# The neighbours' running count by TensorE (row blocks transposed, then multiplied by a constant staircase) in place of a VectorE scan

## The chip, the cores and the metric

The kernel runs on one core of one Trainium2 chip. The metric is the device time of one execution in microseconds (us). TensorE is called PE below, its weight loads PEld, VectorE DVE, ScalarE ACT, GpSimdE POOL; SP and ACT also issue DMAs. Every engine works off its own list of instructions in the order in which the program was built; it never overtakes an instruction that waits.

## The reference, cut to what matters

Sixteen graphs (batch 16) of 1024 nodes with 64 channels go through four graph layers with residuals. `adj` is a float 0/1 matrix per graph. Only layer 0 matters here: it drops some neighbours of a node by their rank, then takes quantiles over the remaining ones.

```python
neigh = (adj_ > 0) & ~eye
ni = neigh.astype(jnp.int32)
rank = jnp.cumsum(ni, axis=-1) - ni            # the running count along a row
nb = ni.sum(-1)
skip = jnp.where(nb > T, (nb + K - 1) // K, 1) # T, K = 10, 2
rem = neigh & (sk > 1) & (rank % sk == sk - 1) & mask[:, :, None]
rem = rem | jnp.swapaxes(rem, 1, 2)
adj_d = jnp.where(rem, 0.0, adj_)              # the neighbours that stay
s = jnp.sort(jnp.where((adj_d > 0)[..., None], x[:, None, :, :], jnp.inf), axis=2)
# agg: weighted quantiles 0.25, 0.5, 0.75 of s, then two dense layers; layers 1 to 3 use the full adj
```

## The kernel before, in words

The graphs are worked through in eight pairs. Of each pair there are five kinds of work:

- **Sort** (`sort_pair`, L720 to L803): the nodes' values are sorted on DVE in 55 compare steps (L729, L736, L737, called *forward steps* here), and 55 *back steps* (L753, L754, L756/L757 or L760) carry codes back to the nodes. The masks between go through DRAM (L740, L749).
- **Preparation** (`neighbours`, L806 to L904): for each graph eight row blocks of 128 nodes, in two halves of four. A block is loaded (L819), compared with 0 into `ni` (fp8, L820), its diagonal cleared by POOL (L821), counted along the row by a scan (`cum`, L825), and the raw block is transposed on PE and stored for the later layers (L831 to L834). After four blocks a chain of ten small DVE instructions (`sk`, L840 to L850) gives each row's skip. Then per block three ACT passes over 1024 columns (L854 Square with the bias `sk[:, 2]`, L855 Square, L856 Relu) give `rem`, 0/1; PE adds up `ni`, `-rem` and `-rem` transposed into `ndT` (L875), and ACT evicts (L881). Every PE result of the preparation goes through two PSUM buffers, `pk`. `ni`, `rem` and `wide` have one buffer, so a pair's second graph starts when its first is through. At the end of a graph PE counts the neighbours that stay (L885) and ten small DVE instructions (L892 to L904) make the quantiles' positions.
- **Selection** (`weights`, `select`): PE multiplies `ndT` by tables made from the sort (`wt`, L921; `comb`, L1043), ACT evicts (L1051, L1098), DVE finds maxima (L1109 to L1122), PE and DVE pick the values (L1143, L1151).
- **Extras** (`extras`): nodes with too many neighbours, until L1315.
- **Layers** (`layers`): the rest of layer 0 and layers 1 to 3 of both graphs, until L1528 and L1530 of each graph.

The program order of the loop is: selection of pair p; extras of p; layers of p; preparation of p+1; sort of p+1; load and normalisation for p+2. A scheduler in the language layer decides the order within each engine's list when the program is built; it may move the sort of a later pair ahead, since its buffers are its own. Selection uses all PSUM banks, so it doesn't overlap the preparation, whose `pk` needs two of them. The selection of p+1 needs `ndT` and the positions of p+1, and `wt`, which follows the sort.

So the trace falls into *mixed* stretches M0 to M8 (preparation with extras and layers; M0 is the start, M8 the end) and *selection* stretches S1 to S8 between them. I let S begin at its first L1043 and end at its last L1143.

Of the kernel before, what the change touches and what calls it, by code (L numbers as in the profile page):

```python
# [42 lines left out]
def gnn_stack(ctx, tc, x, adj, nodemask, w, out):  # L43
# [22 lines left out]
    nc.vector.tensor_copy(ident_b, ident)  # L66
    offdiag = const.tile([P, P], BF16, name="offdiag")
    nc.vector.tensor_scalar(offdiag, ident, -1.0, 1.0, op0=ALU.mult, op1=ALU.add)
    ones_b = const.tile([P, N], BF16, name="ones_b")
    nc.vector.memset(ones_b, 1.0)  # L70
    ones_row = const.tile([1, P], F32, name="ones_row")
    nc.vector.memset(ones_row, 1.0)
# [51 lines left out]
    with tc.tile_pool(name="cd", bufs=1, side="right") as cd:  # L124
        code0 = cd.tile([P, N], U16, name="code0")
        rk = cd.tile([P, N], I32, name="rk")
        nc.gpsimd.iota(rk, pattern=[[1, 32], [32, 32]], base=0, channel_multiplier=0)
        rf = cd.tile([P, N], F32, name="rf")
        nc.vector.tensor_copy(rf, rk)
        wf = cd.tile([P, N], F32, name="wf")  # L130
        nc.vector.tensor_scalar(wf, rf, 1.0 / WL, 0.5 / WL - 0.5, op0=ALU.mult, op1=ALU.add)
        wi = cd.tile([P, N], I32, name="wi")
        nc.vector.tensor_copy(wi, wf)
        nc.vector.tensor_copy(wf, wi)
        nc.vector.scalar_tensor_tensor(rf, wf, float(CODE - WL), rf, op0=ALU.mult, op1=ALU.add)
        nc.vector.tensor_copy(code0, rf)
        nc.sync.dma_start(c0_d, code0)
    halfdown = const.tile([P, 1], F32, name="halfdown")
    nc.vector.memset(halfdown, -1023.5 / 2048.0)

# [308 lines left out]
    def general(gw):  # L449
# [47 lines left out]
        with tc.For_i(0, B, 1) as b:  # L497
            with ExitStack() as per_batch:
# [13 lines left out]
                with (  # L512
                    tc.tile_pool(name="nb1", bufs=1) as nb1,
                    tc.tile_pool(name="nb2", bufs=2) as nb2,
                    tc.tile_pool(name="nbp", bufs=2, space=PSUM) as nbp,
                ):
                    kept = nb1.tile([P, NT, N], BF16, name="kept")
                    notrem = nb1.tile([P, NT, N], BF16, name="notrem")
                    for t in range(NT):
                        a = nb2.tile([P, N], F32, name="a", bufs=3)  # L520
                        nc.sync.dma_start(a, adj[ds(b, 1), t * P : (t + 1) * P, :].rearrange("o p j -> (o p) j"))
                        for q in range(0, NT, 4):
                            pt = nbp.tile([P, 4, P], F32, name="pt")
                            for k in range(4):
                                nc.tensor.transpose(pt[:, k, :], a[:, (q + k) * P : (q + k + 1) * P], ident)
                            nc.scalar.copy(adjT[:, q : q + 4, t * P : (t + 1) * P], pt)
                        ni = nb2.tile([P, N], BF16, name="ni")
                        nc.vector.tensor_single_scalar(ni, a, 0.0, op=ALU.is_gt)
                        nc.vector.tensor_mul(ni[:, t * P : (t + 1) * P], ni[:, t * P : (t + 1) * P], offdiag)
                        cum = nb2.tile([P, N], F32, name="cum")  # L530
                        nc.vector.tensor_tensor_scan(cum, ones_b, ni, 0.0, op0=ALU.mult, op1=ALU.add)

                        nbi = nb2.tile([P, 1], I32, name="nbi")
                        nc.vector.tensor_scalar_add(nbi, cum[:, N - 1 : N], 1.0)
                        nc.vector.tensor_single_scalar(nbi, nbi, 1, op=ALU.logical_shift_right)
                        act = nb2.tile([P, 1], F32, name="act")
                        nc.vector.tensor_scalar(
                            act, cum[:, N - 1 : N], MAX_DEGREE, mask[:, t : t + 1], op0=ALU.is_gt, op1=ALU.mult
                        )
                        sk = nb2.tile([P, 2], F32, name="sk")  # L540
                        nc.vector.tensor_copy(sk[:, 1:2], nbi)
                        nc.vector.scalar_tensor_tensor(sk[:, 0:1], sk[:, 1:2], 1.0, act, op0=ALU.add, op1=ALU.mult)
                        nc.vector.tensor_scalar_add(sk[:, 0:1], sk[:, 0:1], -1.0)
                        nc.vector.tensor_scalar_mul(sk[:, 1:2], sk[:, 0:1], 2.0)
                        r1 = nb2.tile([P, N], BF16, name="r1")
                        nc.vector.tensor_scalar(r1, cum, sk[:, 0:1], None, op0=ALU.is_equal)
                        rem = nb2.tile([P, N], BF16, name="rem")
                        nc.vector.scalar_tensor_tensor(rem, cum, sk[:, 1:2], r1, op0=ALU.is_equal, op1=ALU.add)
                        nc.vector.tensor_mul(rem, rem, ni)
                        nc.vector.tensor_sub(kept[:, t, :], ni, rem)  # L550
                        nc.vector.tensor_scalar(notrem[:, t, :], rem, -1.0, 1.0, op0=ALU.mult, op1=ALU.add)
                    for t in range(NT):
                        at = slice(t * P, (t + 1) * P)
                        pk = nbp.tile([P, NT, P], BF16, name="pk")
                        for j in range(NT):
                            nc.tensor.transpose(pk[:, j, :], kept[:, t, j * P : (j + 1) * P], ident_b)
                        nc.vector.tensor_mul(ndT[:, :, at], pk, notrem[:, :, at])
                        nc.vector.tensor_add(ndT[:, t, at], ndT[:, t, at], ident_b)
                    pn = nbp.tile([P, NT], F32, name="pn", bufs=1)
                    for t in range(NT):  # L560
                        for j in range(NT):
                            nc.tensor.matmul(
                                pn[:, t : t + 1], ndT[:, j, t * P : (t + 1) * P], ones_b[:, 0:1],
                                start=(j == 0), stop=(j == NT - 1),
                            )
                    for k, tau in enumerate(TAUS):
                        nc.vector.tensor_scalar(pos1[:, :, k], pn, tau, 1.0 - tau, op0=ALU.mult, op1=ALU.add)
# [237 lines left out]
    def neighbours(b, ndT, row10, qb, qz, nb, nbp):  # L805
# [7 lines left out]
        ni = wide[:, :, pad:]  # L813
        rem = nb.tile([P, NT, N], F8, name="rem")
        for t0 in range(0, NT, HT):
            cum = nb.tile([P, HT, N], F16, name="cum")
            for t in range(t0, t0 + HT):
                a = nb.tile([P, N], F32, name="a", bufs=2)
                nc.sync.dma_start(a, adj[b, t * P : (t + 1) * P, :])  # L819
                nc.vector.tensor_single_scalar(ni[:, t, :], a, 0.0, op=ALU.is_gt, saturate=False)  # L820
                nc.gpsimd.tensor_mul(  # L821
                    ni[:, t, t * P : (t + 1) * P], ni[:, t, t * P : (t + 1) * P], offdiag, saturate=False
                )

                nc.vector.tensor_tensor_scan(  # L825
                    cum[:, t - t0, :], ni[:, t, :], wide[:, t, pad - 1 : pad - 1 + N], 0.0, op0=ALU.add, op1=ALU.add
                )
                for q in range(0, NT, 4):
                    pt = nbp.tile([P, 4, P], F32, name="pk")
                    for k in range(4):  # L830
                        nc.tensor.transpose(pt[:, k, :], a[:, (q + k) * P : (q + k + 1) * P], ident)  # L831
                    at = nb.tile([P, 4, P], F32, name="at", bufs=3)
                    nc.scalar.copy(at, pt)  # L833
                    nc.scalar.dma_start(  # L834
                        a_d[b % 4, q : q + 4, :, t * P : (t + 1) * P].rearrange("j p n -> p j n"), at
                    )


            sk = nb.tile([P, 4, HT], F32, name="sk")
            nc.vector.tensor_tensor(sk[:, 2, :], cum[:, :, N - 1], ni[:, t0 : t0 + HT, N - 1], op=ALU.add)  # L840
            nbi = nb.tile([P, HT], I32, name="nbi")
            nc.vector.tensor_scalar_add(nbi, sk[:, 2, :], 2.0)
            nc.vector.tensor_single_scalar(nbi, nbi, 2, op=ALU.logical_shift_right)
# [2 lines left out]
            nc.vector.tensor_copy(sk[:, 1, :], nbi)  # L846
            nc.vector.scalar_tensor_tensor(sk[:, 1, :], sk[:, 1, :], 1.0, sk[:, 0, :], op0=ALU.add, op1=ALU.mult)
            nc.vector.tensor_scalar(sk[:, 2, :], sk[:, 1, :], -3.0, 4.0, op0=ALU.mult, op1=ALU.add)
            nc.vector.tensor_scalar_add(sk[:, 1, :], sk[:, 1, :], -1.0)
            nc.vector.scalar_tensor_tensor(sk[:, 3, :], sk[:, 1, :], -1.0, sk[:, 1, :], op0=ALU.mult, op1=ALU.mult)  # L850
            for t in range(t0, t0 + HT):
                k = t - t0
                sq = nb.tile([P, N], F32, name="sq")
                nc.scalar.activation(sq, cum[:, k, :], AF.Square, bias=sk[:, 2, k : k + 1], scale=1.0)  # L854
                nc.scalar.activation(sq, sq, AF.Square, bias=sk[:, 3, k : k + 1], scale=1.0)  # L855
                nc.scalar.activation(rem[:, t, :], sq, AF.Relu, bias=one, scale=-1.0, saturate=False)  # L856

# [791 lines left out]
```

## Time and profile before

| | us |
|---|---|
| median of 3 runs | 5952.29 (5937.49 to 5957.01) |
| the profiled execution, its own time | 5945.84 |
| span of the profiled execution | 5944.1 |
| M0 and S1 | 291.4 and 398.4 |
| M1 to M6, mean | 288.1 |
| S2 to S7, mean | 430.5 |
| M7 and S8 | 273.5 and 399.2 |
| M8 | 270.3 |

How to read it: the span runs from the first to the last instruction of one profiled execution. The stretches add up to the span. S2 to S7 are longer than S1 and S8. M7 is the last stretch that prepares a pair, M8 has extras and layers alone, and S8 has no sort beside it. Over the span DVE is busy 5122.3 us, PE 4397.4, ACT 3817.2 and POOL 181.7.

### The profile page before, as it was taken

To read this page: it belongs to the slowest core of one execution; us is meant where nothing else is said; L and a number is where in the kernel's file an instruction comes from. 1 tells how busy PE (TensorE), PEld (TensorE's weight loads), DVE (VectorE), ACT (ScalarE), POOL (GpSimd) and SP (SyncE) were. 2 spreads that over 40 slices of the span, in tenths; PEclk is the share of its full clock that TensorE was granted. 3 is DMA by queue.
4 is the path that set the end of the run, shared out by engine and by line. 5 is a ranking of instruction groups with operands and counts; after the bars stand their busy time and mean duration, and the time that the engine had idled before them with its cause. 6 is when DMAs were issued, how large, how long until landed. Compare 5 with 4: busy or idle time off the path is not lost. (4 is left out here: it accounts for less than half of the span.)

```text
span 5944.1 us, 114264 instructions
## 1 busy us (share of the span) xinstructions
PE 4397.4 (74%) x45010; PEld 2736.4 (46%) x45010; DVE 5122.3 (86%) x13031; ACT 3817.2 (64%) x5701; POOL 181.7 (3%) x283
## 2 busy tenths in 40 slices
PE   1488677895768858788577885788767886779856
PEld 1355443554435544355434554345443554436542
DVE  9999888998789987999879997798879999567744
ACT  2587647775576855668567665676566776577824
POOL 2000000000000000000000000000000000000000
PEclk5699778997889978899688996899868998789967
DMA  3401364014631146211561115611345013520024
GB/s 126 123 26 37 97 200 127 30 48 120 194 94 34 38 127 212 77 36 44 152 204 55 50 51 150 190 39 48 90 141 172 34 48 97 183 87 19 10 75 139
DMA packets 524419, 568.22 MB, mean 96 GB/s; under 512 B 263808, under 2 KB 413568, under 8 KB 523872
## 3 DMA queue, kind: packets, MB, share of 16 engines
q1 hardware_dynamic: 381472, 476.43, 26.3%
q10 hardware_dynamic: 140064, 81.84, 4.5%
q8 instruction: 355, 5.82, 0.4%
q0 software_dynamic: 2336, 2.57, 0.2%
q14 instruction: 192, 1.57, 0.1%
HBM read 376.95 MB, written 183.76 MB: 94 GB/s over the span
## 5 line engine op out<-in xcount | busy, mean ns | idle before, releaser
L1043 PE MATMUL comb<-wt,ndT 128*128 128x512 fp8e5 x6144 | 1442.3, 387 | 146.7 <-ACT sign L1098 121.7
L1051 ACT ACTIVATE y<-comb,qb 128x512 int16<-128x512 f32 x1152 | 744.1, 718 | 512.4 <-PE comb L1043 510.7
L1043 PEld LDWEIGHTS <-ndT 128*128 128x128 fp8e5 x6144 | 592.5, 99 | 876.8 <-issue 246.3
L1143 PE MATMUL cand<-vtab,sign 128*128 128x48 f16 (+1 forms) x18432 | 669.3, 191 | 54.0 <-DVE agg L1018 36.1
L1143 PEld LDWEIGHTS <-sign 128*128 128x128 fp8e5 x18432 | 645.2, 96 | 111.9 <-issue 51.8
L1098 ACT ACTIVATE sign<-comb,lower 128x1024 fp8e5<-128x1024 int16 (+1 forms) x640 | 696.5, 1088 | 0.0
L1098 ACT ACTIVATE sign<-comb,half 128x1024 fp8e5<-128x1024 int16 (+1 forms) x640 | 691.3, 1080 | 0.0
L1114 DVE TENSOR_TENSOR y<-y 128x512 uint16<-128x512 uint16 (+5 forms) x896 | 672.1, 792 | 8.4 <-PE comb L1096 7.2
L1151 DVE COPY_PREDICATED cand<-w_f,cand 128x256 f32<-128x256 uint16 (+1 forms) x1536 | 535.8, 383 | 75.0 <-PE cand L1143 72.8
L1096 PE MATMUL comb<-ident_b,y 128*128 128x128 bf16 x4608 | 316.9, 222 | 117.2 <-ACT sign L1098 76.8
L833 ACT COPY at<-pk 128x512 f32<-128x512 f32 x256 | 147.5, 586 | 384.5 <-PE pk L831 197.1
L1406 PE MATMUL bank<-adjT,nd 128*64 128x512 f32 x1024 | 307.4, 668 | 90.4 <-DMA adjT<-a_d 88.9
L1096 PEld LDWEIGHTS <-y 128*128 128x128 bf16 x4608 | 292.7, 99 | 145.5 <-issue 144.4
L875 PE MATMUL pk<-minus_b,rem 128*128 128x128 bf16 x1024 | 225.5, 247 | 175.2 <-ACT rem L856 175.1
L1406 PE MATMUL bank<-att,hs 128*64 128x512 f32 x512 | 211.0, 941 | 185.0 <-ACT hs L1522 185.0
L825 DVE TENSOR_TENSOR_SCAN cum<-ni 128x1024 f16<-128x1024 fp8e5 x128 | 295.0, 2306 | 32.6 <-POOL ni L821 23.2
L875 PE MATMUL pk<-ident_b,ni 128*128 128x128 bf16 x1024 | 223.3, 244 | 125.1 <-ACT ndT L881 62.7
L729 DVE TENSOR_TENSOR swapped<-s 128x512 uint16<-128x512 f32 x440 | 302.5, 687 | 5.8 <-ACT s L717 1.6
L737 DVE TENSOR_TENSOR s<-s 128x512 f32<-128x512 f32 (+2 forms) x440 | 289.8, 659 | 0.0
L736 DVE TENSOR_TENSOR s<-s 128x512 f32<-128x512 f32 (+2 forms) x440 | 289.6, 658 | 0.0
L921 DVE TENSOR_SCALAR wt<-node 128x2048 uint8<-128x2048 f16 x224 | 268.0, 1221 | 13.1 <-PE comb L1234 13.0
L831 PE MATMUL pk<-ident,a 128*128 128x128 f32 x1024 | 193.5, 339 | 112.9 <-DMA a<-in_adj_dram 79.8
(323 smaller groups left out, 8258.8 us busy)
## 6 DMA issues: line engine op xcount, KB each, us to landing
adjT<-a_d SPq DMA_DIRECT2D x384, 512.0 KB
a<-in_adj_dram SPq DMA_DIRECT2D x128, 512.0 KB
a_d<-at ACTq DMA_DIRECT2D x256, 256.0 KB
m_d<-swapped SPq DMA_DIRECT2D x104, 512.0 KB
swapped<-m_d SPq DMA_DIRECT2D x104, 512.0 KB
n_d<-nat SPq DMA_DIRECT2D x128, 128.0 KB
x_d<-xr SPq DMA_DIRECT2D x48, 256.0 KB
comb_x<-x_d ACTq DMA_DIRECT2D x24, 512.0 KB
```

The lines of the kernel that those rows point to most:

```text
L729: nc.vector.tensor_tensor(side(swapped[:, k, :], j), hi, lo, op=ALU.is_gt)
L737: nc.vector.tensor_tensor(to_hi, lo, hi, op=ALU.min)
L825: nc.vector.tensor_tensor_scan(cum[:, t - t0, :], ni[:, t, :], wide[:, t, pad - 1 : pad - 1 + N], 0.0, op0=ALU.add, op1=ALU.add)
L875: nc.tensor.matmul(pk[:, n % 4, :], lhs, rhs, start=(n % 4 == 0 and m == 0), stop=(m == len(terms) - 1 and last),)
L1043: nc.tensor.matmul(pw, ndT[:, j, t * P : (t + 1) * P], wt[1 + g8][:, j].rearrange("p w c -> p (w c)"), start=(j == 0), stop=(j == NT - 1),)
L1051: nc.scalar.activation(y[:, 0, chunks, at : at + 8 * d_].rearrange("p q (w d) -> p q w d", d=d_), pw.rearrange("p (w q d) -> p q w d", w=8 ...
L1096: nc.tensor.transpose(pt[:, q - q0, :], y[:, 0, q, :].bitcast(BF16), ident_b)
L1098: nc.scalar.activation(signs[tl][s][:, q0:q1, :], pt.bitcast(I16), AF.Sign, bias=before[s], scale=-1.0, saturate=False,)
L1114: nc.vector.tensor_tensor(v[:, :, :, :n], v[:, :, :, :n], v[:, :, :, n : 2 * n], op=ALU.max)
L1143: nc.tensor.matmul(cand[:, e, at : at + 12 * d_].rearrange("p (d l) -> p d l", l=12), signs[tl][sec][:, chunk, :], tab[:, q, :, half_ * 12 ...
L1151: nc.vector.copy_predicated(v[:, :, :, dst : dst + k], mk.to_broadcast([P, 2, C // 2, k]), v[:, :, :, frm : frm + k])
L1406: nc.tensor.matmul(po[to : to + C, :], lhs, rhs[:, f * HALF : (f + 1) * HALF], start=(j == 0), stop=(j == NT - 1))
```

## The change

The scan goes. The count of a row's neighbours comes from the comparison itself: it is done in two halves of 512 columns, each with an accumulated sum, and the diagonal's own entry is subtracted (a product with the identity, also with an accumulated sum). The running count comes from PE: each 128x128 block of `ni` is transposed by a product with the identity, evicted by ACT to fp8 (`turned`), and multiplied by a constant staircase of 0, 1 and 2, four blocks of a half row accumulating in one PSUM bank. The first Square reads that bank, once for each half row of 512 columns; the second half row's bias also holds the first half's count. `ones_w` and the smaller `ones_b` concern a fallback path (`general`), of which the trace shows nothing running. Two setup instructions and `stairs` are new.

```diff
-            cum = nb.tile([P, HT, N], F16, name="cum")
+            sk = nb.tile([P, 6, HT], F32, name="sk")
             for t in range(t0, t0 + HT):
                 a = nb.tile([P, N], F32, name="a", bufs=2)
                 nc.sync.dma_start(a, adj[b, t * P : (t + 1) * P, :])
-                nc.vector.tensor_single_scalar(ni[:, t, :], a, 0.0, op=ALU.is_gt, saturate=False)
-                nc.gpsimd.tensor_mul(
-                    ni[:, t, t * P : (t + 1) * P], ni[:, t, t * P : (t + 1) * P], offdiag, saturate=False
+                own = ni[:, t, t * P : (t + 1) * P]
+                for h in range(2):
+                    nc.vector.tensor_scalar(
+                        ni[:, t, h * (N // 2) : (h + 1) * (N // 2)], a[:, h * (N // 2) : (h + 1) * (N // 2)], 0.0, 0.0,
+                        op0=ALU.is_gt, op1=ALU.add, accum_out=sk[:, 4 + h, t - t0 : t - t0 + 1], saturate=False,
+                    )
+                eye = nb.tile([P, P], F32, name="eye")
+                nc.vector.scalar_tensor_tensor(
+                    eye, own, 1.0, ident, op0=ALU.mult, op1=ALU.mult, accum_out=sk[:, 3, t - t0 : t - t0 + 1]
                 )
-
-                nc.vector.tensor_tensor_scan(
-                    cum[:, t - t0, :], ni[:, t, :], wide[:, t, pad - 1 : pad - 1 + N], 0.0, op0=ALU.add, op1=ALU.add
-                )
+                nc.gpsimd.tensor_mul(own, own, offdiag, saturate=False)
...
-            sk = nb.tile([P, 4, HT], F32, name="sk")
-            nc.vector.tensor_tensor(sk[:, 2, :], cum[:, :, N - 1], ni[:, t0 : t0 + HT, N - 1], op=ALU.add)
+            own = 4 if t0 == 0 else 5
+            nc.vector.tensor_sub(sk[:, own, :], sk[:, own, :], sk[:, 3, :])
+            nc.vector.tensor_scalar_mul(sk[:, 4:, :], sk[:, 4:, :], 2.0)
+            nc.vector.tensor_add(sk[:, 2, :], sk[:, 4, :], sk[:, 5, :])
...
+            nc.vector.tensor_add(sk[:, 4, :], sk[:, 4, :], sk[:, 2, :])
...
                 sq = nb.tile([P, N], F32, name="sq")
-                nc.scalar.activation(sq, cum[:, k, :], AF.Square, bias=sk[:, 2, k : k + 1], scale=1.0)
+                turned = nb.tile([P, NT, P], F8, name="turned", bufs=2)
+                for q in range(0, NT, 4):
+                    pt = nbp.tile([P, 4, P], F32, name="pk")
+                    for i in range(4):
+                        nc.tensor.matmul(
+                            pt[:, i, :], ni[:, t, (q + i) * P : (q + i + 1) * P], ident_b, start=(i == 0), stop=(i == 3)
+                        )
+                    nc.scalar.activation(turned[:, q : q + 4, :], pt, AF.Copy, saturate=False)
+                for q in range(0, NT, 4):
+                    cum = nbp.tile([P, 4, P], F32, name="pk").rearrange("p k n -> p (k n)")
+                    for j in range(4):
+                        nc.tensor.matmul(
+                            cum[:, j * P :], turned[:, q + j, :], stairs[:, 3 * P : (7 - j) * P],
+                            start=(j == 0), stop=(j == 3),
+                        )
+                    nc.scalar.activation(
+                        sq[:, q * P : (q + 4) * P], cum, AF.Square, bias=sk[:, 2 + q // 2, k : k + 1], scale=1.0
+                    )
                 nc.scalar.activation(sq, sq, AF.Square, bias=sk[:, 3, k : k + 1], scale=1.0)
                 nc.scalar.activation(rem[:, t, :], sq, AF.Relu, bias=one, scale=-1.0, saturate=False)
```

More of the change, by code (lines that the diff above doesn't have):

```diff
@@ L68, in gnn_stack @@
     nc.vector.tensor_scalar(offdiag, ident, -1.0, 1.0, op0=ALU.mult, op1=ALU.add)
-    ones_b = const.tile([P, N], BF16, name="ones_b")
+    ones_b = const.tile([P, P], BF16, name="ones_b")
     nc.vector.memset(ones_b, 1.0)
@@ L137, in gnn_stack @@
         nc.sync.dma_start(c0_d, code0)
+        past_ = cd.tile([P, N], I32, name="past_")
+        nc.gpsimd.iota(past_, pattern=[[1, N]], base=1 - 3 * P, channel_multiplier=-1)
+        stairs = const.tile([P, N], F8, name="stairs")
+        nc.vector.tensor_copy(wf, past_)
+        nc.vector.tensor_scalar(wf, wf, 0.0, 2.0, op0=ALU.max, op1=ALU.min)
+        nc.vector.tensor_copy(stairs, wf, saturate=False)
     halfdown = const.tile([P, 1], F32, name="halfdown")
@@ L518, in general @@
                     notrem = nb1.tile([P, NT, N], BF16, name="notrem")
+                    ones_w = nb1.tile([P, N], BF16, name="ones_w")
+                    nc.vector.memset(ones_w, 1.0)
                     for t in range(NT):
@@ L530, in general @@
                         cum = nb2.tile([P, N], F32, name="cum")
-                        nc.vector.tensor_tensor_scan(cum, ones_b, ni, 0.0, op0=ALU.mult, op1=ALU.add)
+                        nc.vector.tensor_tensor_scan(cum, ones_w, ni, 0.0, op0=ALU.mult, op1=ALU.add)
                         nbi = nb2.tile([P, 1], I32, name="nbi")
```

## The prediction

> **What bounds the kernel now.** I read the page's busy times first, then the same by stretch.
>
> ```profile
> PE 4397.4 (74%) x45010; PEld 2736.4 (46%) x45010; DVE 5122.3 (86%) x13031; ACT 3817.2 (64%) x5701; POOL 181.7 (3%) x283
> ```
>
> DVE leads, but only as an average. The windows view, cut at S1, M4, S5, M7, S8 and M8 (columns: stretch, PE, PEld, DVE, ACT, POOL, granted PE clock, DMA share, GB/s), shows two regimes:
>
> ```profile
> 291.40:689.80 398.40, 344.44 (x4100) 221.35 (x4099) 379.45 (x948) 286.97 (x469) 4.15 (x6) 0.94 0.14 42
> ...
> 2854.90:3137.50 282.60, 187.92 (x1491) 114.45 (x1490) 238.46 (x608) 173.14 (x221) 12.46 (x22) 0.75 0.57 171
> 3137.50:3567.90 430.40, 357.83 (x4139) 227.17 (x4137) 411.85 (x1051) 301.92 (x490) 3.82 (x6) 0.92 0.18 54
> ...
> 5001.10:5274.60 273.50, 185.87 (x1483) 110.81 (x1482) 179.33 (x468) 170.75 (x217) 12.66 (x22) 0.76 0.52 158
> 5274.60:5673.80 399.20, 347.81 (x4122) 220.52 (x4120) 302.81 (x813) 296.21 (x477) 2.03 (x2) 0.94 0.11 29
> 5673.80:5944.10 270.30, 157.05 (x872) 75.55 (x871) 128.88 (x371) 100.66 (x115) 3.21 (x6) 0.65 0.33 105
> ```
>
> S5 has DVE at 96%. S8, without sort, has DVE at 76% and PE at 87% and still takes 399.2. So DVE sets S2 to S7 (mean 430.5), with a floor near 395 under it. Mixed stretches differ: M8 prepares nothing, has no engine above 58%, and takes 270.3. They are a chain of hops through extras and layers. The DVE timeline dates that chain's joints: the extras' end (L1315) and the second graph's last sum (L1530) in M8.
>
> ```profile
> 5752.83 0.72 DVE L1315 COPY_PREDICATED agg<-flag,tr 128x512 f32<-128x512 uint16 x1 [6.42 <-PE tr L1314]
> ...
> 5935.84 0.69 DVE L1530 TENSOR_TENSOR nd<-bank,xs 128x512 f32<-128x512 f32 x1 [4.32 <-PE bank L1528]
> ```
>
> Extras take 79.8 and layers 182.3 there. The same events give 103.3 and 210.3 in M7 (preparation, little sort) and 115.8 and 210.6 in M6 (with sort). Sort lengthens the extras; it doesn't lengthen the layers, preparation does. In M6 and M7 the first graph's L1528 comes about 38 earlier than the second's, and the next S starts right behind it, so the second graph's last 40 us of layers lie inside S.
>
> **What the change does to each engine.** The rows, from the groups by form:
>
> ```profile
> L825 DVE TENSOR_TENSOR_SCAN cum<-ni 128x1024 f16<-128x1024 fp8e5 x128 | 295.0, 2306 | 32.6 <-POOL ni L821 23.2 <-ACT sq L854 9.0
> L1517 DVE SCALAR_TENSOR_TENSOR att<-adjT,top,att 128x1024 f32<-128x1024 f32 x128 | 161.5, 1281 | 22.6 <-ACT att L1516 22.4
> L820 DVE TENSOR_SCALAR ni<-a 128x1024 fp8e5<-128x1024 f32 x128 | 87.2, 686 | 27.0 <-DMA a<-in_adj_dram 25.7 <-PE pk L875 1.0
> ```
>
> - DVE: per block 2.31 + 0.69 go. Two comparisons of 512 columns come. No row shows this form with a sum: 0.35 each if it keeps L820's pace, 0.64 + 0.08 (L1517 halved, and its accumulator read of 84 ns) if it runs like L1517. I take 0.6 each, nearer the second because of the sum, plus 0.3 for the diagonal product (0.28 for 128 columns in L1464). Saving 1.5 per block (1.2 to 2.0), 128 blocks: 190; four more small instructions per half at 0.16 take back 20. The page "VectorE: DVE Perf Modes" (Trainium skill, the perf-mode tier table) gives fp32 tensor_scalar two elements per cycle and is silent on sums; by it the saving would be 2.0.
> - ACT: two copies like L1074 (0.587) and two half Squares like L1421 (512 columns from PSUM, 0.681) replace one Square of 1.148; back to back about 1.3 more per block, 166 in all; the list holds about two table loads fewer per M (L666 and others, 1.28 each).
> - PE: eight 128-column products like L1096 (316.9/4608 = 0.069 each) and 2560 columns of staircase at L1043's pace (1442.3/6144 = 0.235 per 512): 1.7 per block, 220 in all, double at the lowest clock seen.
>
> **What the order makes of it.** I compared the instruction lists of both programs as built. This decides more than the 170 us of DVE.
>
> - *Sort moves.* S2 to S7 held on average 41.5 forward and 27.5 back steps. They now hold 8.2 and 52.2. At 1.85 (L729 + L736 + L737 less overlaps) and 1.61 (L753 + L754 + L760) per step that is 121 before and 99 after.
> - *The layers' remainder leaves S.* All 16 exponentials of a pair now stand before S in ACT's list; 3 to 6 stood inside. With their DVE companions (about 3.1 each) some 16 us of DVE leave S, and 4 of preparation.
> - S thus has 409 - 22 - 16 - 4 = 367 of DVE. S1 (379, no remainder) took 398.4, which scales to 385; S8 less its disturbed start gives 391. I take **392** (385 to 400): a gain of 38.5 for each of S2 to S7.
> - *Preparation moves back.* In PE's list of M5, the first graph's count (L885), which stood right behind the extras, now stands among the second graph's layer-2 products. POOL's clearing of the second graph's buffer and its diagonals (L812, L821) stand behind all four L1440 copies, SP's loads of its last four blocks (L819) among the last adjacency loads (L1399), their 8 evictions and 8 DMAs (L833, L834) after the first graph's last Relu (L1525) on ACT. Behind the second L1525, ACT has the remaining 3.5 blocks, strictly one after another, and PE has turn, staircase, sums of each. Then come the count, L892 to L904 and `wt` on DVE, with 20 forward steps in between, and S waits for `wt`.
>
> So M becomes extras + layers of both graphs + tail.
>
> Extras: 8 blocks and 14 to 22 back steps stood before L1315 in M6 and M7; from M3 on 5 blocks and no back step do. Between 79.8 and 103.3 I take 90 (80 to 100); M1 and M2 keep 28 and 11 back steps, +8 and +4.
>
> Layers: ACT's work in this part is about as before, since less preparation stands there but costs more; PE has some 9 x 2 us more. POOL's L821 now follows the diagonal product too (0.3), and behind it only blocks wait that need the half's `sk` anyway: nothing. 212 (190 to 235).
>
> Tail: per block two PE products' groups and a copy (2.2), staircase and half Squares (2.4), L855 and L856 (2.3), then 34 to 46 sums at the pace of the start stretch's end, where PE was idle in between as it will be here. The windows row of that end:
>
> ```profile
> 229.00:258.00 29.00, 15.34 (x189) 13.50 (x189) 27.02 (x57) 20.30 (x29) 0.08 (x1) 0.66 0.30 82
> ```
>
> There sums started 0.107 apart, so 3.6 to 4.9. Three blocks: 34; the half-done fourth 6; L885 2 (64 products, 176 to 178); 13 forward instructions (0.61), ten small ones and two `wt` (1.22) 12. **54** (40 to 65; DVE's forward steps alone are 36). A rule speaks against the change here: the page "TensorE: Matmul & The Clock Gate" (Trainium skill, "A second HAM failure mode: psum-queue depth-cycling") says that PE idling between groups that cycle through PSUM buffers makes its clock drop between full and half. By full clock throughout the tail would be 46, by half clock throughout 57; the row's 0.66 stands between.
>
> M = 90 + 212 + 54 = 356.
>
> Sum against the profiled execution: M1 to M6 6 x 356 + 12 = 2148 against 1728.5, +419.5. S2 to S7 6 x 392 against 2582.8, -231. M7 (4 blocks in the tail, no forward steps) 88 + 205 + 57 = 350 against 273.5, +76.5. S8 391, -8. M0 and S1: sums of DVE unchanged (12 forward steps more against 16 blocks' saving), but the last blocks again one by one: +8. M8 0. Together **+265**: span 6209, plus 1.7 outside the span 6211; that execution lay 6 below the median, so 6215.
>
> **Rivals.**
>
> - *Faster: preparation stays under the layers.* Place: the second graph's last four blocks. If PE and ACT run them in the waits of the attention part (PE idles 185 us on L1522 in all), the tail is gone except for `wt`, and M = 302. With one M for all stretches the sum above is 6 M + 12 - 1728.5 - 231 + M - 6 - 273.5 = 7 M - 2227 (the -8 and +8 cancel): -113, 5831. It decides where M falls below 318. For it: DVE is at 95% in S, and hops may be shorter than I think. Against: the lists put those blocks behind the last Relu of the layers, and nothing overtakes. 0.09.
> - *Much slower: the ring stalls the layers.* Every block now holds PE twice more (staircase behind the copy, turn behind `pk`). Before, PE waited 175.1 for L856 over 128 blocks, 1.4 each; two new waits of 1.2 to 3 in 9 blocks amid the layers and 4 amid the extras give up to 60 per M. M = 410: +643, 6587. For it: PE is in order and two buffers serve five uses. Against: ACT's load there doesn't rise. 0.13.
> - *No change.* M near 318 by chance. 0.05.
> - That scans remain can be left out: the list after has none in `neighbours`.
>
> **How the numbers follow.** The forecast, tail behind the layers, 0.70, with its own range 6030 to 6390: M 335 to 385 and S 385 to 400, not all at one end. 0.03 lies below it and is still slower. The range 5990 to 6440 leaves out the faster case, no change and half of the stalls. 0.3% is about what a measurement can tell from no change. Faster 0.09, same 0.05, slower 0.86.
>
> **What would show it.** Right: no scan; DVE's sum lower by 150 to 200, ACT's higher by about 165; S2 to S7 near 392 with DVE under 94%; M1 to M6 near 356, with the last L875 and L885 of a pair after the second L1530, and `wt` behind them. DVE's accumulating comparison 0.35 or 0.72. Wrong: L885 of the second graph before the last L1530; S still at 430, so that not DVE but another wait sets it; layers above 235, which would be the stalls.

## The result and the profile after

The kernel after takes 6179.2 us (median; 6175.6 to 6186.1), beside 5946.3 for the kernel before on the same chip: a ratio of 1.0392, 95% interval 1.0370 to 1.0415. The profiled execution took 6176.7, span 6174.8: 230.7 more than the span before.

Lines of `neighbours` up to the running count stand 10 or 11 further down in the file after, those behind it 31: the sums are L906, the second graph's last sum of the layers is L1561, `wt` is L952. The busy times of the page:

```profile
PE 4674.2 (76%) x47058; PEld 2905.9 (47%) x47058; DVE 4991.7 (81%) x13642; ACT 3977.5 (64%) x6072; POOL 169.2 (3%) x284
```

DVE has 131 less, ACT 160 more, PE 277 more. DVE fell from 86% to 81% of a longer span, and no other engine took its place as the bound: PE went from 74% to 76%, ACT stayed at 64%. So what binds now is waiting, and the windows view says where. It is cut at S1, S5, M6, M7 and S8 (columns as before: stretch, PE, PEld, DVE, ACT, POOL, granted PE clock, DMA share, GB/s):

```profile
322.20:723.30 401.10, 345.04 (x4100) 220.36 (x4100) 380.74 (x976) 287.15 (x470) 4.29 (x6) 0.93 0.15 45
4049.30:4454.20 404.90, 346.20 (x4100) 222.47 (x4100) 369.71 (x984) 288.01 (x470) 9.46 (x6) 0.93 0.15 41
4454.20:4796.80 342.60, 234.76 (x1782) 139.34 (x1782) 250.04 (x712) 207.32 (x288) 11.73 (x22) 0.78 0.51 158
5194.60:5524.30 329.70, 230.96 (x1775) 137.27 (x1774) 159.92 (x531) 208.13 (x286) 10.24 (x22) 0.79 0.45 140
5524.30:5898.80 374.50, 334.81 (x4084) 215.21 (x4084) 288.42 (x767) 280.41 (x456) 2.04 (x2) 0.96 0.08 21
```

The second line is S6. S2 to S7 take 400.7 on average instead of 430.5, with DVE at 91 to 94%. M1 to M6 take 344.5 instead of 288.1, with no engine above 78%. By stretches: M0 +31, S1 +3, M1 to M6 +338, S2 to S7 -179, M7 +56, S8 -25, M8 +6: together +231.

The groups by form of the new instructions:

```profile
L872 PE MATMUL pk<-ident_b,ni 128*128 128x128 bf16 x1024 | 115.9, 257 | 85.5 <-ACT at L844 35.7 <-ACT ndT L912 29.5 <-ACT turned L875 10.1
L875 ACT ACTIVATE turned<-pk 128x512 fp8e5<-128x512 f32 x256 | 143.7, 593 | 56.1 <-PE pk L872 55.1 <-ACT at L844 0.5
L883 ACT ACTIVATE sq<-pk,sk 128x512 f32<-128x512 f32 x256 | 169.5, 685 | 133.3 <-PE pk L879 88.5 <-DVE sk L861 43.0 <-DVE sk L863 1.6
...
L830 DVE TENSOR_SCALAR_CACHE_REDUCE ni<-a 128x512 fp8e5<-128x512 f32 x256 | 170.2, 679 | 69.4 <-DMA a<-in_adj_dram 38.8 <-PE pk L906 21.0 <-ACT sq L886 8.7
L830 DVE DVE_READ_ACCUMULATOR ni<-a 128x1 f32 x256 | 20.8, 81 | 0.0
L835 DVE SCALAR_TENSOR_TENSOR eye<-ni,ident 128x128 f32<-128x128 fp8e5 x128 | 36.2, 283 | 0.3
```

Read the releasers: the turn (L872, the transposition on PE) waits for ACT to free a `pk` buffer, `turned` (L875, its eviction) waits for the turn, the half Square (L883) waits for the staircase's products (L879). Each pair is a hop from one engine to the other and back, on queues that also serve the layers.

The end of M6 on ACT, from the timeline (start, duration, what ended the idle time), shows one block alone, from Relu to Relu:

```profile
4750.29 1.15 ACT L887 ACTIVATE rem<-sq,one 128x1024 fp8e5<-128x1024 f32 x1
4752.88 0.77 ACT L912 ACTIVATE ndT<-pk 128x512 fp8e5<-128x512 f32 x2 [1.45 <-PE pk L906]
4755.00 0.60 ACT L912 ACTIVATE ndT<-pk 128x512 fp8e5<-128x512 f32 x1 [1.36 <-PE pk L906]
4755.50 0.59 ACT L875 ACTIVATE turned<-pk 128x512 fp8e5<-128x512 f32 x1
4756.27 0.60 ACT L875 ACTIVATE turned<-pk 128x512 fp8e5<-128x512 f32 x1 [0.19 <-PE pk L872]
4757.78 1.27 ACT L883 ACTIVATE sq<-pk,sk 128x512 f32<-128x512 f32 x2 [0.91 <-PE pk L879]
4759.08 1.15 ACT L886 ACTIVATE sq<-sq,sk 128x1024 f32<-128x1024 f32 x1
4760.26 1.15 ACT L887 ACTIVATE rem<-sq,one 128x1024 fp8e5<-128x1024 f32 x1
```

Ten microseconds for one block, with ACT idle for 3.9 of them (the bracketed waits). The sums of one block and three whole blocks go through like this behind the layers' last sum (Relus at 4750.3, 4760.3, 4769.8 and 4779.5), and then comes DVE's short work for `wt`:

```profile
4749.24 0.69 DVE L1561 TENSOR_TENSOR nd<-bank,xs 128x512 f32<-128x512 f32 x1 [0.68 <-PE bank L1559]
...
4786.44 0.17 DVE L923 TENSOR_SCALAR last<-pk 128x8 f32<-128x8 f32 x1 [6.36 <-PE pk L916]
...
4794.43 3.48 DVE L952 TENSOR_SCALAR wt<-node 128x2048 uint8<-128x2048 f16 x3
```

DVE has done all that stands ahead of L923 in its list and is idle for 6.36 us until the count (L916) comes. The chain of blocks sets this end, not DVE.

The slow blocks are not only there. In M6 before, the Relus of the first graph's eight blocks lie within 54 us; after, within 109.

### The profile page after: what moved, and what is told of

The parts are those of the page before. It is cut to its first block, busy times and chain, and to the rows that moved or that the text cites. A ratio compares the mean times of both kernels' runs of the same rounds, so it can differ in the third digit from the quotient of the medians.

```text
span 6174.8 us, 119206 instructions
## 1 busy us (share of the span) xinstructions
PE 4674.2 (76%) x47058; PEld 2905.9 (47%) x47058; DVE 4991.7 (81%) x13642; ACT 3977.5 (64%) x6072; POOL 169.2 (3%) x284
## 4 chain that ended last, share of the span: by engine, by line
PE 39%; ACT 25%; DVE 20%; DMA 11%; issue 3%; SPq 1%; ACTq 0%; POOL 0%; DVEq 0%; POOLq 0%
PE comb L1074 12%; ACT sign L1129 7%; PE cand L1174 6%; DMA adjT<-a_d 4%; PE bank L1437 4%; PE comb L1265 3%; DVE y L1145 3%; ACT y L1082 3%; PE pk L906 3%; DMA a_d<-at 2%; PE pk L879 2%; DVE cand L1182 2%; ACT sq L886 2%; ACT sq L883 1%; ACT rem L887 1%
## 5 line engine op out<-in xcount | busy, mean ns | idle before, releaser
L1074 PE MATMUL comb<-wt,ndT 128*128 128x512 fp8e5 x6144 | 1457.5, 390 | 219.4 <-ACT sign L1129 124.0
L906 PE MATMUL pk<-minus_b,rem 128*128 128x128 bf16 x1024 | 252.4, 267 | 158.8 <-ACT rem L887 158.7
L906 PE MATMUL pk<-ident_b,ni 128*128 128x128 bf16 x1024 | 254.1, 261 | 110.8 <-ACT sq L883 103.7
L912 ACT ACTIVATE ndT<-pk 128x512 fp8e5<-128x512 f32 (+3 forms) x352 | 160.3, 479 | 199.5 <-PE pk L906 196.8
L1437 PE MATMUL bank<-att,hs 128*64 128x512 f32 x512 | 202.7, 902 | 110.9 <-ACT hs L1553 110.2
L952 DVE TENSOR_SCALAR wt<-node 128x2048 uint8<-128x2048 f16 x224 | 261.5, 1217 | 23.5 <-PE comb L1265 23.4
```

Source lines behind the costliest of these rows:

```text
L906: nc.tensor.matmul(pk[:, n % 4, :], lhs, rhs, start=(n % 4 == 0 and m == 0), stop=(m == len(terms) - 1 and last),)
L1074: nc.tensor.matmul(pw, ndT[:, j, t * P : (t + 1) * P], wt[1 + g8][:, j].rearrange("p w c -> p (w c)"), start=(j == 0), stop=(j == NT - 1),)
L1437: nc.tensor.matmul(po[to : to + C, :], lhs, rhs[:, f * HALF : (f + 1) * HALF], start=(j == 0), stop=(j == NT - 1))
```

## The experiments

Three theories at the start: A, the order in which the program is built puts the second graph's last blocks behind the layers, and that tail is the loss; B, the added work on PE and ACT is paid wherever it stands; C, DVE's accumulating comparison eats the gain. D and E come later. The kernels also differ in built order, since every edit moves it. Ratios are to the kernel before on the same chip (5952 to 5954 beside these runs), with 95% intervals.

### The preparation ahead of the layers: `order`

```
 if pr + 1 < pairs:
-    made = prepare(pr + 1, nb, nbp)
+    with tc.high_priority():
+        made = prepare(pr + 1, nb, nbp)
```

> Edit: in the loop over pairs the preparation is issued under high priority, nothing else. In the built order the second graph's count (L917) then stands before the layers' last sum (L1562), and some 17 more forward steps and a few of the layers' companions lie in S again. Theory A (the loss is the built order: the second graph's last blocks one after another behind the layers): the tail of 47 falls to about 10, M from 344 to about 300; S goes back from 400 to about 425, since DVE gets some 25 us of steps and 15 of layer work back there; total about 6030 (5960 to 6110). Theory B (the added work on PE and ACT itself holds up whatever it is mixed with): the tail goes, but extras and layers grow by as much, M stays at 340 or above, S grows too, total above 6200. Theory C (the slower accumulating comparison on DVE): no term of it changes, total within 1% of after's.

6260.8 us, 1.0512 (1.0490 to 1.0533): slower than after, though the tail is gone. Its M6 and S7:

```profile
4524.70:4845.90 321.20, 224.53 (x1721) 133.51 (x1720) 205.68 (x610) 189.03 (x263) 8.85 (x20) 0.79 0.47 142
4845.90:5283.50 437.60, 363.16 (x4163) 230.56 (x4162) 413.12 (x1087) 306.10 (x496) 5.36 (x8) 0.93 0.19 57
```

The second count now ends 100 before M does, and M falls from 344 to 318 only: extras take 120 instead of 96, layers 233 instead of 201 (means of M2 to M6). S goes to 440 with DVE at 94%; the layers' remainder and some 17 forward steps are in it again. Theory A as a tail falls: in this order the tail is gone, and more than it cost appears in the extras, the layers and S. Theory B's total (above 6200) holds, its M (340 or above) doesn't.

### No running count at all: `free`

```
-turn, two copies, staircase (PE L872, L879; ACT L875)
-nc.scalar.activation(sq[half], cum, AF.Square, ...)
+nc.scalar.activation(sq[half], ni[:, t, half], AF.Square, ...)
```

> Leaves out the running count (turn, copies, staircase); the first Squares read the 0/1 neighbours, so the output is not the reference's, and the fallback branch is switched off. All of DVE's part of the change stays. Theory A: with nothing added on PE and two copies less per block on ACT, the preparation lies under the layers again (built order: second count before the last sums), M about 290 and S about 392 with DVE at 91 to 94%, total about 5760 (5680 to 5850), which is what the removal of the scan alone is worth. Theory B says the same. Theory C (accumulating comparison, eye and the small steps eat the gain): total at 5900 or above, M above 310.

5833.3 us, 0.9792 (0.9773 to 0.9811), near the upper end of what theories A and B gave. Without the running count, which this kernel leaves out, DVE's part is thus worth 120 us, although DVE's sum is 170 lower (5122.3 to 4951.9), and the running count on PE costs 346. Theory C's bound of 5900 is not reached.

### The accumulating comparison alone: `sums`

```
-nc.vector.tensor_single_scalar(ni[:, t, :], a, 0.0, op=ALU.is_gt, ...)
+for h in range(2):
+    nc.vector.tensor_scalar(ni[half], a[half], 0.0, 0.0,
+        op0=ALU.is_gt, op1=ALU.add, accum_out=sums[...], ...)
 (scan kept)
```

> The kernel before with one part of the change alone: the comparison in two halves with sums; the scan stays. DVE gets 128 x (2 x (0.68 + 0.08) - 0.69) = 106 us more. Theory A: DVE binds S, not M, and the comparisons lie in M; built order has 9 forward and 37 back steps in M and 50 and 20 in S, so S about 430, M 290 to 305, total 5950 to 6060, about 6000. Theory C: at least the 106 us and the delay of what waits for the comparison, 6060 to 6150. Theory B: no change within 0.5%, since PE and ACT get nothing.

5962.5 us, 1.0019 (1.0003 to 1.0035). The comparison costs what it did inside the change:

```profile
L822 DVE TENSOR_SCALAR_CACHE_REDUCE ni<-a 128x512 fp8e5<-128x512 f32 x256 | 170.4, 676 | 7.3 <-DMA a<-in_adj_dram 6.8 <-PE pk L880 0.5
```

The comparisons and their accumulator reads take 104 more, DVE's sum rises by 78 (5122.3 to 5200.5), and 9 of it reach the total. That lies in A's range and in B's 0.5%. Theory C is out: DVE is busy for 79 to 88% of M1 to M6 here, so M has DVE to spare.

### The turn earlier: `early`

```
 (first loop, behind the transposition of block t)
+turn of block t, copies to turned[:, t - t0]
 (second loop)
-turn, copies
```

> After, with each block's turn and its two copies moved into the first loop (behind the block's own transposition), so that four turned blocks wait in buffers and the second loop's chain has only staircase, Squares, Relu and sums left. Theory A: the chain per block falls from 9.5 to about 7.3, so the tail from 47 to about 40, M from 344 to about 336, S unchanged at 400; total about 6120 (6080 to 6180). Theory B: the same work, no change, within 0.5% of after's 6179. Theory C: no change.

6118.8 us, 1.0270 (1.0251 to 1.0290): 60 less with the same instructions, as theory A said. But the tail did not get shorter (M3 to M6: 45 to 49); the extras did (88 to 91 instead of 95 to 97), M0 by 6, and S2 to S7 by 2.5 each. So the amount of work doesn't decide alone, nor does the tail as such.

### The staircase left out, and the copies on DVE: `turn_only`, `turn_dve`

```
 turn_only:
-staircase; Square reads cum
+Square reads turned
 turn_dve:
-nc.scalar.activation(turned[...], pt, AF.Copy, ...)
+nc.vector.tensor_copy(turned[...], pt, ...)
```

> After with the staircase left out: the half Squares read the turned blocks, so the output is not the reference's, and the fallback branch is switched off. PE keeps the turn, ACT all its instructions; the built order still leaves 2.5 to 3.5 blocks behind the layers. Theory A (order: what counts is the length of the chain in the tail): the chain per block loses some 2, the tail 6 to 7, total about 6130. Theory B, as it stands after the run with the preparation ahead (what is added on PE and ACT in the mixed stretches is paid nearly in full wherever it is put, since PE and ACT wait for each other there): 0.94 x 16 = 15 per mixed stretch and the same in M0, total about 6060 (6030 to 6090).

> After with the two copies of the turned blocks moved from ACT to DVE; the same hops, PE's work unchanged, ACT 144 less, DVE some 150 more. Theory A (the hops count, not who does them): M no shorter, total 6160 to 6220. Theory B, ACT's part of it: 18 less per mixed stretch, as DVE is at 73% there, total about 6060 (6020 to 6100).

`turn_only` 6097.8 us, 1.0252 (1.0224 to 1.0279): 81 less than after, between the two forecasts. `turn_dve` 6159.6 us, 1.0339 (1.0321 to 1.0356): taking 136 us from ACT (3977.5 to 3841.8) brought 20. That is the lower end of A's forecast: moving the hop to another engine changed little. DVE's sum rose by as much (4991.7 to 5127.3), though, and no run tells whether that hid a gain from ACT.

### The turned blocks from POOL: `from_at`

```
 nc.scalar.copy(at, pt)
+nc.gpsimd.tensor_single_scalar(turned[:, t - t0, q : q + 4, :], at, 0.0, op=ALU.is_gt)
 ...
-turn, copies
+nc.gpsimd.tensor_mul(turned[:, t - t0, t, :], ..., offdiag)
```

> After without turn and copies: the turned blocks are made on POOL (nearly idle) by comparing the evicted transposes `at` with 0, in the first loop; the staircase and the half Squares stay. Per block PE has 0.55 and ACT 1.18 less, and the `pk` ring two uses less. The built order still leaves 3 to 3.5 blocks behind the layers, and POOL has some 256 comparisons more. Theory B: 16 x 1.73 = 28 less per mixed stretch, total about 5985 (5950 to 6030). Theory A: only the tail gets shorter, as with the early turn or a little more, total about 6100 (6070 to 6130).

6023.5 us, 1.0120 (1.0093 to 1.0147), near B's forecast: 156 less. But it removes the work and a hop out of each block's chain at once, and it makes the turned blocks in the first loop, which in `early` was worth 60 alone. POOL takes 1617 ns for half a block, and the staircase's weight loads wait only 7 us for POOL in the whole run. The next run looks at the work alone.

### The turn added to the kernel before: `turn_add`

```
 nc.scalar.activation(sq, cum[:, k, :], AF.Square, ...)   # scan kept
+turn of block t, two copies to turned   (nothing reads them)
```

> The kernel before, scan kept, with the turn of each block and its two copies added behind the first Square; nothing reads the copies. So PE gets 0.55 and ACT 1.18 more per block and `pk` two more uses, but no instruction waits for their result. In the built order the second graph's count still stands before the layers' last sums. Theory B (added work on PE and ACT is paid wherever it is put, as PE's in-order queue stands at each hop): about as much as its removal gave with the comparison on POOL, 156, so 6110 (6080 to 6150). Theory D (the work lies in the waits of the mixed stretch as long as the preparation ends before the layers do; what is paid is only a preparation that ends after them): 5960 to 6030.

5915.9 us, 0.9939 (0.9922 to 0.9955): not slower at all, and a little faster than before. Theory B is out for the turn: its products and copies, with both uses of `pk`, fit into waits that were there. Its M6 and S7:

```profile
4259.90:4544.20 284.30, 193.52 (x1628) 120.49 (x1626) 228.30 (x606) 189.07 (x257) 12.73 (x22) 0.78 0.58 176
4544.20:4973.80 429.60, 355.14 (x4131) 223.28 (x4130) 405.85 (x1014) 301.01 (x487) 4.04 (x7) 0.94 0.16 49
```

ACT has 189 in M6 here and 175 before, and M6 is no longer. Not every stretch is like M6: M1 takes 313.5 instead of 284.7, and the mean of M1 to M6 is 291.8 instead of 288.1; S2 to S7 take 422.1 instead of 430.5. The gain thus lies in S, and no part of the edit takes work away there, so the built order, which the edit changed, is the likely cause; no run isolates it.

### One graph ahead: `after_hi0`, `fa_hi0`, `fa_count_hi0`

```
+with tc.high_priority() if pr and i == 0 else ExitStack():
     neighbours(pr * 2 + i, *made[i], nb, nbp)
 fa_hi0:        the same, on from_at
 fa_count_hi0:  besides, counts = turned blocks x ones on PE;
                one whole comparison, no sums, no diagonal product
```

> After with the preparation of each pair's first graph under high priority and the second's not; nothing else. In the built order the first count then stands inside the early layers and the second among the layers' last sums; 13 back steps return from S to M, 19 forward steps go from M to S. Theory D: both preparation and layers end together, tail near 10, M 315 to 325, S about 408, total 6060 (6020 to 6110). Theory B: as with the whole preparation ahead, 6180 to 6260.

> The comparison on POOL in place of turn and copies, with the first graph's preparation under high priority. Theory D: the tail of 14 to 30 that was left goes, M 300 to 305, S about 405, total 5940 (5900 to 5980). Theory B: no work is saved, so within 0.5% of the 6024 without the priority.

> As the run before, and the counts of neighbours come from PE (the turned blocks times a column of ones, 32 products of one column for half a graph) in place of the sums of DVE's comparison, which is one whole instruction of 0.69 again, without the diagonal product. DVE 128 x 1.1 = 140 less, PE some 16 x 1.2 = 20 more. Theory C (DVE's slower comparison is part of the loss): 90 to 140 less than the run before. Theory D (DVE isn't what mixed stretches wait for; S gains only what sort moves into M): 20 to 60 less, about 5900.

`after_hi0` 6020.6 us, 1.0107 (1.0085 to 1.0130): after's very instructions in another order, 159 faster. M falls to 308, S is 414. The total is the lower end of theory D's, with a shorter M and a longer S than it gave; B's 6180 to 6260 is missed. In M2 to M6 the second graph's count now comes 18 or 19 us before S begins and the layers' last sum 5 or 6 after, so the tail is gone. With `order` that makes three orders of one set of instructions: 6261, 6179, 6021. `fa_hi0` 6042.8 us, 1.0157 (1.0139 to 1.0175): no gain, against theory D's 5940 and within theory B's 0.5% of 6024. M fell from 320 to 302, and S rose from 402 to 424. `fa_count_hi0` 6114.4 us, 1.0274 (1.0250 to 1.0298): slower by 72, though DVE's sum is 126 lower than in `fa_hi0` (5040.6 to 4914.3). Its counts need PE, a `pk` buffer and a hop to DVE before any Square of the half can start. But M1 to M6 hardly differ (303.6 and 302.1); the time lies in S2 to S7 (431.4 and 424.2) and M7 (318.8 and 282.4). So less work on the busiest engine went with more time, against theories C and D both, and that the longer chain is the cause isn't shown.

### The work kept, the dependence cut: `loose`

```
 turn, copies, staircase as in after
-nc.scalar.activation(sq[half], cum, AF.Square, ...)
+nc.scalar.activation(sq[half], ni[:, t, half], AF.Square, ...)
```

> After with every instruction of the running count kept on PE and ACT (turn, copies, staircase, two half Squares), but the half Squares read the 0/1 neighbours instead of the staircase's result; the output is not the reference's, and the fallback branch is switched off. What goes is the dependence alone: Squares, Relu and sums no longer stand behind turn, copy and staircase of their block. The built order puts the second count among the layers' last sums by itself. Theory E (the loss is the longer chain of each block, and the order that it leads to; the added work itself is nearly free, as the run with the turn added to the kernel before shows): M about 300, S about 402, total 5870 (5820 to 5930), near the 5833 without any of the work. Theory B (PE's and ACT's added work): no shorter than the best order of the same work so far, 6020 or more.

5848.9 us, 0.9816 (0.9799 to 0.9834). Its interval just overlaps that of `free` (0.9773 to 0.9811), which has none of the work. M6 and S7:

```profile
4214.40:4518.50 304.10, 209.42 (x1775) 122.83 (x1774) 232.73 (x708) 204.68 (x288) 10.45 (x22) 0.85 0.56 169
4518.50:4913.50 395.00, 340.30 (x4110) 218.86 (x4111) 380.16 (x989) 288.54 (x472) 4.93 (x6) 0.96 0.17 49
```

ACT has 204.7 in M6, beside 207.3 after, in 38 us less. Around the sixth block of M6, ACT goes on without a wait, and `turned` goes where there is room:

```profile
4289.86 1.15 ACT L887 ACTIVATE rem<-sq,one 128x1024 fp8e5<-128x1024 f32 x1
4291.05 1.33 ACT L883 ACTIVATE sq<-ni,sk 128x512 f32<-128x512 fp8e5 x2
4292.28 0.74 ACT L912 ACTIVATE ndT<-pk 128x512 fp8e5<-128x512 f32 x2
4292.92 1.14 ACT L886 ACTIVATE sq<-sq,sk 128x1024 f32<-128x1024 f32 x1
4293.96 0.59 ACT L912 ACTIVATE ndT<-pk 128x512 fp8e5<-128x512 f32 x1
4294.44 0.60 ACT L875 ACTIVATE turned<-pk 128x512 fp8e5<-128x512 f32 x1
4294.91 1.16 ACT L887 ACTIVATE rem<-sq,one 128x1024 fp8e5<-128x1024 f32 x1
```

Relu to Relu takes 5.1 here; the same two Relus are 16.2 apart in M6 after, and those of the block shown above 10.0. The first graph's eight Relus of M6 lie within 51 us again. The second graph's, amid the layers, do not draw together (122 us, 115 after, 97 before). Theory E holds: of the 346 that the running count costs, 330 go with the dependence (6179 less 5849) and 16 with the work.

M0 shows the chain almost by itself, since no extras and no layers run beside it, and it is as long in all three orders of after (321 to 323). The windows view of M0 in after, `loose` and `free`:

```profile
0.00:322.20 322.20, 127.82 (x938) 93.82 (x939) 273.03 (x715) 125.52 (x194) 48.26 (x80) 0.63 0.39 120
0.00:289.00 289.00, 111.89 (x938) 81.24 (x939) 254.59 (x685) 122.17 (x194) 48.10 (x80) 0.77 0.43 128
0.00:273.30 273.30, 83.91 (x682) 66.82 (x683) 248.30 (x676) 106.78 (x162) 48.43 (x80) 0.58 0.44 133
```

The dependence costs 33 there and the work 16. The last four Relus of M0 are 9.6 to 10.6 apart after and 4.1 to 5.5 before. (DVE also does forward steps of the next pair there: 13 after, 3 in `loose`, none in `free`.) So the longer chain costs time where no layers stand in its queues. As an estimate, 33 for each of the eight preparations would be 266 of the 330.

Two things stay open. `loose` also lets the staircase's `pk` buffer go without waiting for the Square, so the longer chain and the longer hold of two shared buffers are not told apart. And its built order differs, as in every run; how much of the loss in M1 to M7 is the chain itself and how much the order that goes with it isn't settled, beyond the 240 between the slowest and the fastest order of after's own instructions.

## Why the prediction was right, and where it was not

The time lay 36 below the forecast of 6215 and on its side. (The forecast's last sum, 6211 and 6, gives 6217.) Part of that closeness is luck, since errors of both signs cancel: against the forecast S2 to S7 were 52 longer, M0 with S1 26 and M8 6, while M1 to M6 were 81 shorter, M7 20 and S8 17. Steps in turn:

- **DVE.** Forecast 150 to 200 less, measured 131. The mis-sized term is the accumulating comparison: 0.6 each assumed, measured 0.679 plus 0.081 for the accumulator, above the upper of its two bounds (0.72). 256 of them cost 191 instead of 154. Two small terms: the diagonal's product cost 46 with its accumulator read instead of 38, and the small instructions are three more per half, not four (13642 DVE instructions instead of 13031). The page "VectorE: DVE Perf Modes" (Trainium skill, the perf-mode tier table) gives fp32 tensor_scalar two elements per cycle; the whole comparison of before keeps twice the pace of this one (686 for 1024 columns, 679 for 512), so with a sum that pace isn't reached here. For the total time it hardly mattered, as `sums` shows.
- **ACT and PE.** ACT +160 against 166. PE's busy time +277 against 220 of issue time.
- **Selection.** S2 to S7 400.7 against 392, just above the range of 385 to 400: DVE's work in S was 370 to 378 instead of 367, and its share 91 to 94% instead of S1's 95%. Over six stretches +52.
- **Mixed stretches.** 344.5 against 356. M2 to M6 by terms: extras 96 (90), layers 201 (212), tail 46 (54). Blocks in the tail took 9.6 to 10, not 11.3, and DVE's end with `wt` and start 10, not 12. M0 was missed the other way, +31 against +8 for M0 and S1 together: DVE was taken to set the start, and its share of M0 fell from 93% (271 of 291.4) to 85% (273 of 322.2): the chain's blocks went as slowly there as in the tail.
- **The clock.** The tail's working took 0.66; the windows view of M6's tail (4749.3 to 4786.4) has 0.77. The page "TensorE: Matmul & The Clock Gate" (Trainium skill, "A second HAM failure mode: psum-queue depth-cycling") reports, for one kernel whose matmul groups cycle through PSUM banks, that the clock swung between half and full as PE idled briefly between the groups: 0.77 lies between, but the sums of the first block there start 0.107 apart, as at 0.66. M0 took as long at a mean clock of 0.81 (`order`, 322.8 us) as at 0.63 (after, 322.2).
- **The cause.** Here the prediction was half right. It saw that the last blocks run strictly one after another, and priced that. It took their place behind the layers for the whole reason, and that holds only in part. `after_hi0` has no tail and wins back 159 of the 233; `order` has none either and loses 82 more. What goes further is the longer chain itself, as `loose` and M0 show. The price of the rival "preparation stays under the layers" (5831) held S at 392, but the overlap hands the layers' remainder back to S: `order` had M 318 and S 440, `after_hi0` M 308 and S 414. The stalls rival (layers above 235) did not show in after (201). `order` came near its sign, with layers of 233 and extras of 120, but not by the waits that the rival names: PE's waits at the turn and the staircase were 70 us over that run and 110 after, while its wait for the layers' `hs` was 207.5 and 110.2. What lengthens the layers there isn't settled. The work itself, 220 on PE and 166 on ACT, the prediction put at little in the layers and priced in the tail as links of a chain; `loose` bears that out, with 16 for all of it.

## What to carry to other kernels

Relief for the busiest engine can be bought with latency when the replacement goes back and forth between two others: count the hops that a block's result must make, not only the busy time they add. Where in-order queues are shared with another chain, test the two apart by keeping every instruction and cutting only the dependence, and by adding the instructions to the old kernel with nobody waiting for them. And where a scheduler lays out the queues, an edit's effect includes the order it causes: the same instructions differed here by 4%.

## What was not expected of the hardware

A comparison that also sums takes 679 ns for 512 fp32 columns where the plain one takes 686 for 1024. POOL's comparison of 512 fp32 columns into bf16 takes 1617 ns, per column nearly five times as long as DVE's plain one. In `from_at` POOL is busy with them for 411 us, and that kernel is still 156 faster than after:

```profile
L846 POOL TENSOR_SCALAR turned<-at 128x512 bf16<-128x512 f32 x256 | 411.5, 1617 | 344.9 <-ACT at L845 342.6 <-issue 2.0
```
